# Sparse attention in batches of two key tiles, with the tensor engine's half-row work kept together

## The chip, the core and the metric

The kernel runs on one core of a Trainium2 chip. The metric is device time in microseconds (us), the median of three runs. The kernel before takes 2334.74 us (2334.36 to 2340.01). The profile is one execution of it, 2307.7 us from its first to its last instruction. Engines: PE does matrix products (PEld are its weight loads), DVE and ACT work on vectors, POOL issues the gathers, SP issues plain transfers.

## What is computed

One layer of attention over a graph, followed by a mixture of experts. Cut to what matters here:

```python
# x: 4096 x 512, adj: 4096 x 4096 of 0 and 1, 8 heads of 64
adj = maximum(adj, eye)
q, k, v = (einsum('nd,hdk->hnk', layernorm(x), W) for W in (Wqs, Wks, Wvs))
scores = einsum('hqk,hmk->hqm', q, k) * kd ** -0.5
scores = scores + 0.01 * eye - 1e16 * (1.0 - adj)
att = softmax(scores, axis=-1)
x = x + einsum('hqm,hmk,hko->qo', att, v, Wo)
x = x + experts(layernorm(x))     # the best 2 of 8 experts for each row
```

adj has few ones, unevenly spread. For each tile of 128 queries the kernel lists the keys that any of them uses, packs them into tiles of 128 keys and works only on those. All arithmetic is in float32.

## The kernel before

Stages: projections and lists; attention; the end of the routing; experts. The attention is the stage that the change touches.

A tile of queries has its own tile of keys (c = -1) and listed[i] tiles of listed keys. A listed tile counts for all 128 queries, or for one half of them (64) when its keys are used by that half alone (half_of is None, 0 or 1). A step handles one tile of keys for one tile of queries. Names: `kv` holds keys and values as gathered (128 keys x 1024), `kT` the keys turned so that heads lie on the rows, `s` the scores in PSUM, `e` their exps, `mask` the gathered part of adj, `po` the sum of values, `acc` the sum of exps.

```python
def turn(n):                       # transposes on PE, 64 rows each
    pk = ps_k.tile([P, 2, TB], F32, tag="k")          # ps_k: 1 buffer
    for p in range(NP):                               # NP = 4 pairs of heads
        for r in range(2):
            half = slice(r * KD, (r + 1) * KD)        # KD = 64
            nc.tensor.transpose(pk[:, r, ts(p, KD)], kv[n][half, ts(p, P)], ident[half, half])
    nc.scalar.copy(kT[n]..., pk...)                   # ACT

def scores(n):
    ...
    if full:                                          # 128 queries: 8 products in half rows
        s = [ps_s.tile([P, NP, P], F32, tag="s") for r in range(2)]   # ps_s: 3 buffers
        for p in range(NP):
            for r in range(2):
                rows = slice(r * KD, (r + 1) * KD)
                nc.tensor.matmul(s[r][:, p, :], k[rows, p, :], q_in[i][rows, p, r, :], ...)
        for r in range(2):
            nc.scalar.activation(e..., s[r], AF.Exp)
    else:                                             # 64 queries: 4 products in full rows
        s = ps_s.tile([P, NP, 2, QH], F32, tag="s")   # q_in holds zeros off its diagonal
        for p in range(NP):
            nc.tensor.matmul(s[:, p], k[:, p, :], q_in[i][:, p, :, q], ...)
        nc.scalar.activation(e, s..., AF.Exp)

def masked(n):
    nc.vector.tensor_mul(e, e, m...)                  # DVE

def values(n):
    for h in range(H):                                # 8 products, 128 rows by 64 columns
        p, r = divmod(h, 2)
        nc.tensor.matmul(po[i][r * KD : (r + 1) * KD, p, q], v[:, ts(h, KD)], e[:, h, :], ...)
    if c >= 0:
        nc.vector.tensor_add(acc[i][:, :, q], acc[i][:, :, q], e)

for n, (i, c) in enumerate(items):
    begin()                                           # vector parts of the last step's job
    fetch(n + AHEAD)                                  # AHEAD = 9: kv and mask, 10 buffers
    ...
    if c < 0 and i:
        nc.scalar.copy(osb[i - 1], po.pop(i - 1))     # ps_o: 1 buffer
    turn(n + 3)
    scores(n + 2)                                     # with their exps
    values(n)
    later(n)                                          # pieces of ends of tiles, gate jobs
    masked(n + 2)
```

The ends of a tile (`piece`) are: k=1 `sums` (sums of exps over keys), k=2 their reciprocal, k=3 `rb` (the reciprocals spread to all rows), k=4 the scaled `o`, k=5 `py` (the product with Wo), k=6 the sum with x and its layer norm. Gate jobs, one at a time, turn the row (`pt_b`), multiply it with the gate's weights (`pg`, `pl`), rank the experts and place the rows.

Of the kernel before, what the change touches and what calls it, by code (L numbers as in the profile page):

```python
# [43 lines left out]
def kernel(  # L44
# [165 lines left out]
    AHEAD = 9  # L210
    items = [(i, c) for i in range(NT) for c in range(-1, listed[i])]
# [7 lines left out]
    def load_q(i):  # L219

        q_in[i] = q_two[i % 2]
        for r in range(2):
            rows = slice(r * KD, (r + 1) * KD)
            nc.sync.dma_start(out=q_in[i][rows, :, r, :], in_=qT_d[rows, :, ts(i, P)])
# [8 lines left out]
    def gather_mask(m, i, c):  # L233
        if half_of(i, c) is None:
            gather(m, adjT_rows, mask_of, i, c)
        else:
            gather(m[:, :QH], adjT_halves, mask_of, i, c)
# [4 lines left out]
    def mask_part(m, i, c):  # L242
        return m if half_of(i, c) is None else m[:, :QH]

    def fetch(n):

        i, c = items[n]
        kv[n] = kvp.tile([P, KV], F32, tag="kv", name=f"kv_{i}_{c}")
        mask[n] = kvp.tile([P, P], F32, tag="mask", name=f"mask_{i}_{c}")
        if c < 0:  # L250
            nc.sync.dma_start(out=kv[n], in_=kv_d[ts(i, P), :])
            nc.sync.dma_start(out=mask[n], in_=adjT[i, ts(i, P), :])
            return
        gather(kv[n], kv_d, key_of, i, c)
        if (i, c) in packed:
            nc.sync.dma_start(out=mask_part(mask[n], i, c), in_=packed_at(i, c))
        else:
            gather_mask(mask[n], i, c)

        if waiting and n % 3 == 0:  # L260
            waiting.pop(0)[1]()
# [9 lines left out]
    with tc.tile_pool(name="wqkv", bufs=1) as wp, tc.tile_pool(name="p1", bufs=3) as work, tc.tile_pool(  # L271
# [353 lines left out]
        def pack():  # L625
            i, c = ready.pop(0)
            m = work.tile([P, P], F32, tag="mask", bufs=5, name=f"pm_{i}_{c}")
            gather_mask(m, i, c)
            packed[i, c] = len(packed)
            nc.sync.dma_start(out=packed_at(i, c), in_=mask_part(m, i, c))  # L630
# [4 lines left out]
        for u in range(8 * NTB + 1):  # L635
# [38 lines left out]
            if u - 3 in load_at:  # L674
                neighbours(load_at[u - 3])
                if load_at[u - 3] == NT - 1:

                    ap_cm.__exit__(None, None, None)
                    kv_cm = tc.tile_pool(name="kv", bufs=AHEAD + 1, side="right")
                    kvp = kv_cm.__enter__()  # L680
                    q_cm = tc.tile_pool(name="q", bufs=1, side="right")
                    qp = q_cm.__enter__()
                    q_two = [qp.tile([P, NP, 2, P], F32, name=f"q_{k}") for k in range(2)]
                    for t in q_two:
                        for r in range(2):
                            rows = slice(r * KD, (r + 1) * KD)
                            nc.gpsimd.memset(t[rows, :, 1 - r, :], 0.0)
                    load_q(0)
                    fetch(0)
            if u == 8 * NTB - 4:  # L690
                for n in range(1, AHEAD):
                    fetch(n)
# [172 lines left out]
    with tc.tile_pool(name="p2a", bufs=2) as two, tc.tile_pool(  # L865
# [30 lines left out]
        x_in, kT, es, po, acc = {}, {}, {}, {}, {}  # L896
# [7 lines left out]
        def load_x(i):  # L904
            x_in[i] = two.tile(
                [P, D], F32, tag="last" if i == NT - 1 else "xt", bufs=1, name=f"xr_{i}"
            )
            nc.sync.dma_start(out=x_in[i], in_=x[ts(i, P), :])

        def turn(n):  # L910
            kT[n] = work.tile([P, NP, P], F32, tag="kT", bufs=3, name=f"kT_{n}")

            pk = ps_k.tile([P, 2, TB], F32, tag="k", name=f"pk_{n}")
            for p in range(NP):
                for r in range(2):
                    half = slice(r * KD, (r + 1) * KD)
                    nc.tensor.transpose(  # L917
                        pk[:, r, ts(p, KD)], kv[n][half, ts(p, P)], ident[half, half]
                    )
            nc.scalar.copy(  # L920
                kT[n].rearrange("k p (r j) -> k r p j", r=2),
                pk[:, :, : NP * KD].rearrange("k r (p j) -> k r p j", p=NP),
            )
# [4 lines left out]

        def scores(n):

            i, c = items[n]
            full = half_of(i, c) is None
            q = queries(i, c)
            k = kT.pop(n)
            if c < 0:
                e = two.tile([P, H, P], F32, tag="acc", name=f"acc_{i}")
                acc[i] = e
            else:
                e = work.tile([P, H, P], F32, tag="e", name=f"e_{i}_{c}")
                if not full:  # L940
                    e = e.rearrange("p h q -> p (h q)")[:, : H * QH]
                    e = e.rearrange("p (h q) -> p h q", h=H)
            es[n] = e
            if full:

                s = [
                    ps_s.tile([P, NP, P], F32, tag="s", name=f"s{r}_{i}_{c}") for r in range(2)
                ]
                for p in range(NP):
                    for r in range(2):  # L950
                        rows = slice(r * KD, (r + 1) * KD)
                        nc.tensor.matmul(  # L952
                            s[r][:, p, :], k[rows, p, :], q_in[i][rows, p, r, :],
                            start=True, stop=True,
                        )
                for r in range(2):
                    nc.scalar.activation(  # L957
                        e.rearrange("p (a r) q -> p r a q", r=2)[:, r], s[r], AF.Exp
                    )
            else:  # L960

# [490 lines left out]
```

## Time and profile before

| part | value |
|---|---|
| median of 3 runs | 2334.74 us |
| span in the profile | 2307.7 us |
| PE busy in the span | 2102.1 us (91%) |
| DVE, ACT, POOL busy | 1266.7, 933.3, 1030.9 us |
| projections and lists | 0 to 462 us |
| attention | 462 to 1693 us |
| end of the routing | 1693 to 1760 us |
| experts | 1760 to 2307.7 us |

How to read it: a row of the profile names the line of the kernel, the engine, the operation, what is written and what is read, and the shape. L917 are the transposes, L920 their copy, L952 the scores of 128 queries and L964 those of 64, L957 and L967 the exps, L975 the mask, L987 the values, L993 the sum of exps, L1012 `sums`, L1025 `rb`, L1034 `py`, L702, L708 and L721 the gate's products, L1150 the copy of `po`, L228 the gathers. "64*128" ahead of a shape is the part of PE's array that is used, rows by columns. A float32 product appears as two records of a load and a matmul each, a transpose as one. The end of a matmul is modelled, so distances between starts tell more than durations. The granted clock is PE's, as a share of its full speed.

### The profile page before, as it was taken

How to read it: one execution, taken by the hardware profiler on the slowest of the kernel's cores; microseconds unless marked ns; L12 is line 12 of the kernel's file. 1: busy time of each engine (PE TensorE's matmuls, PEld its weight loads, DVE VectorE, ACT ScalarE, POOL GpSimd, SP SyncE). 2: the span in 40 equal slices, each digit the busy share in tenths (PEclk: the TensorE clock that was granted, in tenths of full speed). 3: DMA queues.
4: the chain of work that ended last, by engine and by line, in shares of the span. 5: the costliest groups of instructions: out<-in, count | busy, mean ns of one | idle time of the engine just before them, and what ended most of it. 6: DMA issues, size and time to landing. Idle time of an engine off the chain costs nothing. (4 is left out here: it accounts for less than half of the span.)

```text
span 2307.7 us, 48617 instructions
## 1 busy us (share of the span) xinstructions
PE 2102.1 (91%) x18796; PEld 1389.0 (60%) x18796; DVE 1266.7 (55%) x2297; ACT 933.3 (40%) x1709; POOL 1030.9 (45%) x1080
## 2 busy tenths in 40 slices
PE   7988897899999889999999999998957999999998
PEld 3434443387777777777777777776733444444444
DVE  4686676166666656656656666665652332323332
ACT  2644443355445445445445454544421222222221
POOL 1044434667666566565555655566521121212112
PEclk9998999899999999999899999999978999999999
DMA  7777877667777777778777877767666656665564
GB/s 293 313 264 269 273 261 248 207 192 212 225 242 233 221 235 234 220 219 234 211 234 223 237 220 225 224 197 225 186 237 148 134 137 136 137 138 134 137 132 91
DMA packets 214383, 481.13 MB, mean 208 GB/s; under 512 B 49234, under 2 KB 81234, under 8 KB 210052
## 3 DMA queue, kind: packets, MB, share of 16 engines
q0 software_dynamic: 79232, 242.18, 37.1%
q1 hardware_dynamic: 133764, 233.68, 33.0%
q8 instruction: 153, 2.51, 0.4%
q10 hardware_dynamic: 1152, 2.10, 0.3%
q14 instruction: 82, 0.67, 0.1%
HBM read 400.43 MB, written 77.42 MB: 207 GB/s over the span
## 5 line engine op out<-in xcount | busy, mean ns | idle before, releaser
L228 POOL DMA_INDIRECT kv<-kv_d,key_of x363 | 405.8, 1118 | 384.4 <-PE po L987 220.5
L975 DVE TENSOR_TENSOR e<-e,mask 128x512 f32<-128x512 f32 (+1 forms) x363 | 322.3, 888 | 308.1 <-ACT e L967 144.3
L920 ACT COPY kT<-pk 128x512 f32<-128x512 f32 x395 | 232.3, 588 | 370.6 <-PE pk L917 216.6
L987 PE MATMUL po<-e,kv 128*64 128x64 f32 (+1 forms) x5808 | 322.4, 250 | 18.2 <-issue 17.9
L1387 POOL DMA_INDIRECT out_dram<-y,r x71 | 110.6, 1558 | 473.7 <-ACT y L1386 453.2
L993 DVE TENSOR_TENSOR acc<-acc,e 128x512 f32<-128x512 f32 (+1 forms) x363 | 320.5, 883 | 2.5 <-PE sums L1012 0.9
L228 POOL DMA_INDIRECT mask<-in_adjT_dram,mask_of x234 | 282.3, 1206 | 72.9 <-issue 63.4
L987 PEld LDWEIGHTS po<-e,kv 128*64 128x64 f32 x5808 | 251.9, 139 | 70.1 <-issue 25.8
L964 PE MATMUL s<-q,kT 128*128 128x128 f32 x1832 | 276.2, 295 | 3.1 <-issue 2.7
L1351 PE MATMUL ph<-w,xT 128*128 x568 | 257.9, 597 | 0.7 <-ACT xT L207 0.7
L1380 PE MATMUL py<-w,hT 128*128 x568 | 255.6, 593 | 0.9 <-DVE hT L1365 0.9
L964 PEld LDWEIGHTS s<-q,kT 128*128 128x128 f32 x1832 | 230.8, 197 | 19.4 <-issue 3.5
L917 PE MATMUL pk<-ident,kv 64*128 64x64 f32 x2904 | 177.5, 239 | 49.0 <-ACT kT L920 30.1
L917 PEld LDWEIGHTS pk<-ident,kv 64*128 64x128 f32 x2904 | 123.9, 141 | 120.2 <-issue 72.0
L228 POOL DMA_INDIRECT pm<-in_adjT_dram,mask_of x129 | 126.2, 978 | 149.6 <-DMA packed_h<-pm 80.0
L957 ACT ACTIVATE e<-s 128x512 f32<-128x512 f32 x268 | 146.9, 597 | 72.1 <-PE s L952 30.1
L1385 DVE TENSOR_TENSOR y<-py,bb 128x512 f32<-128x512 f32 x71 | 49.1, 692 | 225.6 <-PE py L1380 225.6
L967 ACT ACTIVATE e<-s 128x512 f32<-128x512 f32 x229 | 137.9, 602 | 79.4 <-PE s L964 43.9
L359 DVE TENSOR_REDUCE flags<-adjT 128x64 f32<-128x4096 f32 x32 | 141.0, 4408 | 52.3 <-DMA adjT<-in_adjT_dram 52.3
L1351 PEld LDWEIGHTS ph<-w,xT 128*128 128x128 f32 x568 | 103.1, 192 | 103.8 <-issue 102.7
L1380 PEld LDWEIGHTS py<-w,hT 128*128 128x128 f32 x568 | 102.5, 190 | 104.0 <-issue 102.8
L952 PE MATMUL s<-q,kT 64*128 64x128 f32 x2144 | 160.2, 283 | 4.6 <-issue 2.6
(598 smaller groups left out, 2614.8 us busy)
## 6 DMA issues: line engine op xcount, KB each, us to landing
adjT<-in_adjT_dram SPq DMA_DIRECT2D x32, 2048.0 KB
bb<-in_L_ffn_b_dram SPq DMA_DIRECT2D x142, 256.0 KB
r<-xs_d SPq DMA_DIRECT2D x71, 258.0 KB
kv_d<-kv SPq DMA_DIRECT2D x32, 512.0 KB
xt<-in_x_dram SPq DMA_DIRECT2D x32, 256.0 KB
qT_d<-qT SPq DMA_DIRECT2D x8, 1024.0 KB
q<-qT_d SPq DMA_DIRECT2D x64, 128.0 KB
xr<-in_x_dram SPq DMA_DIRECT2D x32, 256.0 KB
```

What stands on the lines that cost most here:

```text
L228: nc.gpsimd.indirect_dma_start(out=to, out_offset=None, in_=src, in_offset=bass.IndirectOffsetOnAxis(ap=of[:, at[i] + c : at[i] + c + 1], ...
L359: nc.vector.tensor_reduce(flags[g][:, :, j, :], adj_in.pop(i).rearrange("p c (h q) -> p h c q", h=2), axis=AX.X, op=ALU.max,)
L917: nc.tensor.transpose(pk[:, r, ts(p, KD)], kv[n][half, ts(p, P)], ident[half, half])
L920: nc.scalar.copy(kT[n].rearrange("k p (r j) -> k r p j", r=2), pk[:, :, : NP * KD].rearrange("k r (p j) -> k r p j", p=NP),)
L952: nc.tensor.matmul(s[r][:, p, :], k[rows, p, :], q_in[i][rows, p, r, :], start=True, stop=True,)
L957: nc.scalar.activation(e.rearrange("p (a r) q -> p r a q", r=2)[:, r], s[r], AF.Exp)
L964: nc.tensor.matmul(s[:, p], k[:, p, :], q_in[i][:, p, :, q], start=True, stop=True)
L975: nc.vector.tensor_mul(e, e, m.unsqueeze(1).to_broadcast(e.shape))
L987: nc.tensor.matmul(po[i][r * KD : (r + 1) * KD, p, q], v[:, ts(h, KD)], e[:, h, :], start=(c < 0 and p == 0), stop=(c == listed[i] - 1), s ...
L993: nc.vector.tensor_add(acc[i][:, :, q], acc[i][:, :, q], e)
L1351: nc.tensor.matmul(ph, xTs[b][:, c, :], w1[:, bass.ds(es[b], 1), c, :], start=(c == 0), stop=(c == DC - 1),)
L1380: nc.tensor.matmul(py, hTs[b][:, c, :], w2[:, bass.ds(es[b], 1), c, :], start=(c == 0), stop=(c == HC - 1),)
```

## The change

Two tiles of keys form a batch. Two listed tiles for 64 queries each, one for the first half of the queries and one for the second where there are such, become one unit with 128 columns of scores; tiles for 128 queries stay units of one. A batch is one paired unit, or two of the others. PE then changes less often between products in half rows (transposes, scores) and in full rows or columns (values, ends of tiles). For that the scores of 64 queries go from four products in full rows with zeros in q to eight in half rows, and q loses its zeros. Two keys share one copy of kT. The copy of po follows the last values of its tile. The core of the diff, with cuts marked:

```diff
-    AHEAD = 9
-    items = [(i, c) for i in range(NT) for c in range(-1, listed[i])]
+    KEPT = 10
+    units, batches = [], []
+    for i in range(NT):
+        parts = {h: [c for c in range(listed[i]) if half_of(i, c) is h] for h in (0, None, 1)}
+        pairs = [[a, b] for a, b in zip(parts[0], parts[1])]
+        ...
+        wide = [[-1]] + [[c] for c in parts[None]]
+        ...
+        wide = [wide[j : j + 2] for j in range(0, len(wide), 2)]
+        pairs = [[pair] for pair in pairs]
...
-        def turn(n):
-            kT[n] = work.tile([P, NP, P], F32, tag="kT", bufs=3, name=f"kT_{n}")
+        def turn(batch):
+            k = work.tile([P, 2, NP, P], F32, tag="kT", bufs=2, name=f"kT_{batch[0]}")
+            ...                      # transposes of both keys, then one copy on ACT
...
         def scores(n):
+            for r in range(2):
+                s = ps_s.tile([P, NP * P], F32, tag="s", name=f"s{r}_{n}")
+            for j, c in enumerate(cs):
+                for p in range(NP):
+                    for r in range(2):
+                        rows = slice(r * KD, (r + 1) * KD)
+                        nc.tensor.matmul(
+                            ss[n][r][:, p, ts(j, m)], k[rows, p, :],
+                            q_in[i][rows, p, queries(i, c)], start=True, stop=True,
+                        )
-                for p in range(NP):
-                    nc.tensor.matmul(
-                        s[:, p], k[:, p, :], q_in[i][:, p, :, q], start=True, stop=True
-                    )
...
         def values(n):
+            if last:
+                osb[i] = single.tile([P, NP, P], F32, tag="o", name=f"o_{i}")
+                nc.scalar.copy(osb[i], po.pop(i))
...
-        LAST = 6
+        LAST = 4                     # products of k=1, 2, 3 in later(b); their reads in begin(b)
...
-        for n, (i, c) in enumerate(items):
-            begin()
-            fetch(n + AHEAD)
-            turn(n + 3)
-            scores(n + 2)
-            values(n)
-            later(n)
-            masked(n + 2)
+        for b, batch in enumerate(batches):
+            begin(b)
+            fetch(k0 + KEPT)         # k0: the batch's first key
+            ...
+            for n in batch[: 0 if own else None]:
+                summed(n)            # acc, taken out of values
+            for n in nxt:            # the next batch
+                scores(n)
+                exps(n)
+                if n == nxt[0] and b + 2 < len(batches):
+                    turn(batches[b + 2])
+                masked(n)
+            for n in batch:
+                if own:
+                    summed(n)
+                values(n)
+            later(b)
```

The other stages are the same in both kernels.

## The prediction

> **What bounds the kernel now.** I read four views in this order. The table by windows splits the span into stages, with the edges taken from the first and last start of the values' matmuls and of the expert blocks. Columns: stretch, its length, busy time of PE, PEld (weight loads), DVE, ACT, POOL, then granted clock, DMA share, GB/s.
>
> ```profile
> 462.00:1693.00 1231.00, 1142.58 (x15377) 920.43 (x15375) 798.96 (x1243) 606.96 (x1206) 741.17 (x639) 0.97 0.74 219
> 1760.00:2307.70 547.70, 538.21 (x1665) 264.99 (x1663) 165.88 (x348) 127.68 (x208) 110.64 (x71) 1.00 0.58 131
> ```
>
> The first row is the attention, 1231 of 2308 us, and the only stage that the change touches: PE is busy 93% of it, DVE 65%, POOL 60%, ACT 49%. So PE's stream sets the pace, and I go to its timeline for the price of each phase. A phase costs the distance from its start to the start of the next (the printed duration has a tail that overlaps the next phase).
>
> ```profile
> 1109.28 0.69 PE L987 MATMUL po<-e,kv 128*64 128x64 f32 x16
> 1109.90 0.46 PE L917 MATMUL pk<-ident,kv 64*128 64x64 f32 x8
> 1110.29 1.16 PE L964 MATMUL s<-q,kT 128*128 128x128 f32 x8
> 1111.38 0.69 PE L987 MATMUL po<-e,kv 128*64 128x64 f32 x16
> ...
> 1123.89 0.47 PE L917 MATMUL pk<-ident,kv 64*128 64x64 f32 x8
> 1124.19 1.11 PE L952 MATMUL s<-q,kT 64*128 64x128 f32 x16
> 1125.23 0.69 PE L987 MATMUL po<-e,kv 128*64 128x64 f32 x16
> ```
>
> Read off: a step on 64 queries is values 0.62, transposes 0.39, scores 1.09 = 2.10 us. A step on 128 queries has transposes 0.30 and scores 1.04; its values are in the same timeline at 1101.46 with the next phase at 1102.49, so 1.03, together 2.37. There are 229 of the first (363 listed tiles less the 134 whose mask product is 128x1024) and 134 + 32 own tiles = 166 of the second. The ends of a tile, from the same timeline: sums 0.58, rb 1.09, transposes of the output 0.59, gate 0.36 and 0.32; py is 120.1 us busy for 32 tiles, 3.75 each: 6.7 in all. Sum: 229 x 2.10 + 166 x 2.37 + 32 x 6.7 = 481 + 393 + 214 = 1088 us. The stage takes 1231, so **some 143 us are lost** in waits and in stretches at half clock (a phase that follows a long wait takes about twice its usual time). By the waits, PE and its loads wait most for ACT's copy of po (15.5 us, and 19.4 for the loads) and of kT (22.1 and 28.8).
>
> Third, what is fixed in a phase and what grows with the work. Values on 64 columns cost 0.62, on 128 columns 1.03. The loads in the 0.69 us phase start 0.059 us apart per pair (0.55 us less one load's 0.137, over 7 steps), so 8 pairs are 0.47 and 0.15 is fixed. The timeline of the loads gives the scores:
>
> ```profile
> 1108.18 0.19 PEld L952 LDWEIGHTS s_-1_12111<-q,kT 64*128 64x128 f32 x1
> 1108.18 0.19 PEld L952 LDWEIGHTS s_-1_12112<-q,kT 64*128 64x128 f32 x1
> 1108.30 0.19 PEld L952 LDWEIGHTS s_-1_12111<-q,kT 64*128 64x128 f32 x1
> 1108.30 0.19 PEld L952 LDWEIGHTS s_-1_12112<-q,kT 64*128 64x128 f32 x1
> 1108.41 0.19 PEld L952 LDWEIGHTS s_-1_12111<-q,kT 64*128 64x128 f32 x1
> ```
>
> The two halves of the rows load at the same instant, and a new pair comes each 0.11 us: 8 pairs are 0.88. The rest, 0.16 for 128 queries and 0.21 for 64, is fixed. The transposes' loads come 0.06 per pair (0.33 less 0.139, over 3): 0.24 for 4 pairs, so 0.06 is fixed if scores in half rows follow and 0.15 if scores in full rows do. The whole fixed part is then 0.15 + 0.21 + 0.15 = 0.51 us in a step on 64 queries and about 0.37 in one on 128.
>
> **What the Trainium skill says.** "TensorEngine Tiling (Array Packing)", section Tiling Modes, says that a change of tiling mode, not of the tile alone, drains the engine. The trace agrees: the same eight transposes cost 0.39 ahead of full rows and 0.30 ahead of half rows, 0.09 for the drain. "TensorE: Matmul & The Clock Gate", section LDWEIGHTS, puts a load at its columns over 1.2, whatever its rows; for 128 columns 107 ns, and the trace shows 0.11 us a pair. Its section on the clock gate says that a long idle spell halves PE's clock, which fits the mean of 0.97 here and 0.67 in the stretch of waits after this stage. "PSUM — Partial Sum Buffer", section on bank collisions, lets two row tiles not write one bank at a time, which explains why a half-row product takes two of the three score banks.
>
> **The change part by part.** The 395 keys become 207 batches. Counting them with the code: 102 pairs of half tiles in one unit, 78 of two 128-query units (32 with the own tile), 8 mixed, 19 of one key.
>
> *Pair batch, PE alone.* Scores in half rows: 16 matmuls, each of two records, are 16 pairs of records. They now have 64 columns, not 128, but a pair still loads 128 columns of kT, so I keep 0.11: 1.76, plus 0.10 to enter the mode. Eight pairs of transposes 0.48, drain 0.09, values 16 x 0.059 + 0.15 = 1.09. Sum 3.52 against 2 x 2.10 = 4.20: **0.68 saved**, all of it fixed parts. The scores themselves save nothing.
>
> *Pair batch, with ACT.* The new order is scores(b+1), exps(b+1), transposes(b+2), copy kT(b+2), then values(b), and the next scores need that copy. ACT's queue is in order, so the copy waits for both exps. From the start of the last score: 0.30 to the first exp (in the timeline above the last pair starts at 1124.19 + 0.05 + 7 x 0.11 = 1125.01, and ACT's exp stands at 1125.33), then 0.5 from one to the next, as three neighbours on ACT show:
>
> ```profile
> 1109.94 0.60 ACT L957 ACTIVATE acc<-s_-1_12111 128x512 f32<-128x512 f32 x1
> 1110.43 0.59 ACT L957 ACTIVATE acc<-s_-1_12112 128x512 f32<-128x512 f32 x1
> 1110.96 0.59 ACT L920 COPY kT<-pk 128x512 f32<-128x512 f32 x1
> ```
>
> So 0.30 + 1.0, and the copy is 128x1024 now. From 0.27 for 128 elements and 0.59 for 512 I estimate 0.17 + 1024 x 0.83 ns = 1.0, and 0.05 back to PE: 2.35. PE has 0.11 + 0.48 + 0.09 + 1.09 = 1.8 to do meanwhile, so it **waits 0.55** unless ends fill the gap. The gain is 0.1 plus the ends E of that batch, at most 0.68. One third of pair batches (32) carry rb (1.09): 22 us. Gate pieces (0.3 to 0.6) fall in about half of the other 70: 35 x 0.5 = 18. The last 35 give 4. Sum 44.
>
> *Wide batch.* Scores 0.10 + 0.88, transposes 0.48, scores 0.05 + 0.88, drain 0.09, values 16 x 0.109 + 0.15 = 1.89: 4.37 against 2 x 2.37. But the second scores need a fourth bank of three, free only after the first exp: 0.30 + 0.60 + 0.05 = 0.95 after the last score, and PE arrives at 0.65. So 4.67, 0.07 saved, 78 times: 5. Mixed ones give some 3. One-key batches on 64 queries (17) lose about 0.5 to ACT's chain: -8. **Regular part: 44 us off.**
>
> *What else moves.* The copy of po now directly follows a tile's last values, and the next tile's values come a whole scores phase later: the wait of 35 us on PE and its loads should go, and some half clock with it; I take 50 of the 143. DVE gets one product of 1.22 for two of 0.69, twice per pair batch: 0.32 x 102 = 33 us, off the path. Against it: fetches now come two at a time and are needed two batches later, about 11 us, where before they had six steps (6 x 3.1 = 18.7). POOL needs 3.8 us to issue two, DMA some 5 for 1 MB at 219 GB/s. It fits, not by much; and the half tiles' scores have twice the records. I put 20 us on both.
>
> Sum: 44 + 50 - 20 = 74, so 2334.74 - 74 = about 2260.
>
> **The rivals.** (1) *ACT's chain takes all:* with a slower copy or exps held up behind other ACT work, pair batches come to 4.2 or more, and gain and loss cancel: 2300 to 2335. ACT's 49% busy speaks against; the strict order of exps before the copy speaks for. (2) *The loads end behind need:* DMA share 0.74 would become 0.79 at the shorter stage, and the slack falls by 7 us; PE would wait for kv in many batches, 2320 or more. Against it: no wait of PE for a kv transfer is listed now, and POOL is idle 40% of the stage. (3) *PE gets its full saving:* if scores on 64 columns cost less than 0.11 a pair, or ends fill all gaps, regular gain is 102 x 0.68 + 78 x 0.37 = 98, with 50 from waits 148: about 2190.
>
> **Range and chances.** 2260 with 2205 to 2315: the low end is most of rival 3, the high end most of rival 1. The 2% mark is 2288. I give 0.70 for faster, 0.23 within, 0.07 slower; the gain's parts are independent, and two of them would have to fail.
>
> **What would show it.** Half scores at 0.11 us a pair: right if 16 pairs take 1.7 to 1.9. The wait of PE for ACT's kT copy should grow to 20 us or more in total and be the longest of its list; that for the po copy should nearly vanish. The copy should read 1.0 us. DVE should be busy about 30 us less. PE waits for kv would show rival 2. I am wrong if the stage ends above 1210 us (the waits stayed) or under 1090 (scores were cheap).

## The result, and the profile after

The changed kernel takes 2448.21 us (median of 6; 2442.64 to 2465.52) beside 2334.32 us for the kernel before on the same chip (6 runs): a ratio of **1.0509, 95% interval 1.0468 to 1.055**. The ratios, here and below, are those on record, made from the single executions; they differ a little from quotients of the medians. Predicted were 2260 us, 2205 to 2315. The change is slower by 114 us where it should have been 74 faster.

One fact is needed for all that follows. The kernel before took 2305 to 2340 us in this comparison and in three later ones (two of them on one chip), and 2171 to 2190 us in four others, each on a chip of its own; nothing in the kernel differed. I call them the slower and the faster chips, though no run tells whether the chip itself or something else at work on it makes the difference. Every ratio below is to the kernel before on the same chip.

The stage of attention, in the view by windows (window, length, busy us and instructions of PE, its loads, DVE, ACT and POOL, mean granted clock, DMA share, GB/s), now reads:

```profile
464.00:1831.00 1367.00, 1191.06 (x17177) 999.15 (x17175) 787.34 (x1044) 565.35 (x1037) 712.37 (x632) 0.89 0.64 196
```

It was 1231 long at a clock of 0.97; it is 1367 at 0.89. These 136 us, and 18 more between the last values and the first product of the experts (51.4 before, 69.6 after), make up 154 of the 156 us by which the two profiled runs differ (spans of 2307.7 and 2463.6). The timeline of PE shows what happens inside:

```profile
869.89 1.15 PE L1020 MATMUL po<-e,kv 128*64 128x64 f32 x32
870.97 2.00 PE L973 MATMUL s<-q,kT 64*128 64x64 f32 x32
872.81 0.49 PE L937 MATMUL pk<-ident,kv 64*128 64x64 f32 x10
873.70 0.36 PE L937 MATMUL pk<-ident,kv 64*128 64x64 f32 x4 [0.40 <-issue]
874.45 0.28 PE L937 MATMUL pk<-ident,kv 64*128 64x64 f32 x2 [0.39 <-issue]
874.65 1.10 PE L1020 MATMUL po<-e,kv 128*64 128x128 f32 x9
875.97 2.18 PE L1020 MATMUL po<-e,kv 128*64 128x128 f32 x23 [0.21 <-issue]
878.31 3.68 PE L973 MATMUL s<-q,kT 64*128 64x64 f32 x32 [0.15 <-ACT kT L942]
881.77 0.53 PE L937 MATMUL pk<-ident,kv_-1_8366 64*128 64x64 f32 x6
```

The first two lines are as priced: values of two half tiles take 1.08 us to the next phase, 16 pairs of half-row scores 1.84. Then the 16 transposes break into groups of ten, four and two, with idle time in between for which no semaphore accounts ("issue"), and the next two phases take about twice their price: 32 values 3.66 in place of 1.90, and the same 32 scores 3.46 in place of 1.84. The windows over this stretch, cut where the clock can change, show the reason:

```profile
868.92:872.33 3.41, 3.41 (x70) 3.27 (x72) 3.41 (x4) 1.85 (x4) 1.16 (x2) 1.00 0.89 266
872.33:875.75 3.42, 2.51 (x37) 1.72 (x35) 1.10 (x2) 0.00 (x0) 2.81 (x3) 1.00 1.03 314
875.75:879.16 3.41, 3.04 (x32) 2.60 (x33) 1.74 (x2) 2.10 (x3) 1.99 (x2) 0.50 0.64 238
879.16:882.57 3.41, 3.41 (x44) 3.41 (x42) 0.71 (x1) 0.56 (x2) 2.18 (x3) 0.50 0.60 173
882.57:885.99 3.42, 3.42 (x50) 3.19 (x48) 2.65 (x3) 1.43 (x3) 1.52 (x2) 0.50 0.98 289
885.99:889.40 3.41, 2.89 (x48) 2.30 (x46) 1.00 (x1) 1.20 (x2) 2.43 (x3) 1.00 1.03 267
```

The clock is the third number from the end of a line. The slot from 872.33 holds the gaps; PE is busy 2.51 of its 3.41 us. The next three slots run at 0.50. The view of waits for the stage says how much of each there is:

```profile
PE po L1020 <- issue: 58.0, 119, 1.2
PE pk L937 <- issue: 26.9, 55, 1.1
PE s L973 <- ACT kT L942: 23.9, 32, 1.9
PE s L973 <- ACT e L986: 23.0, 27, 2.1
PE s L973 <- issue: 15.0, 29, 2.1
```

Columns: who waits for what, us in total, times, longest. The waits for ACT are those that were foreseen; "issue" comes to 100 us, where before had 42.5 (18.9 + 18.3 + 2.7 + 2.6). Four lines of before:

```profile
PE pk L917 <- ACT kT L920: 22.1, 24, 3.2
PE pk L917 <- issue: 18.9, 41, 1.8
PE po L987 <- issue: 18.3, 48, 1.1
PE po L987 <- ACT o L1150: 15.5, 18, 3.5
```

To have sums, I split PE's stage by its phases: the "own price" is the first decile of the durations of phases of one kind; the excess is put to gaps of over 0.32 us inside the phase, then to half clock (half of the time spent under it), and the rest to waits at a change of phase. All in us; the last two columns are the same kernels on a faster chip (experiment 2).

| | before | after | before, faster chip | after, faster chip |
|---|---|---|---|---|
| own price | 1073 | 1010 | 1076 | 999 |
| gaps inside a phase | 42 | 155 | 1 | 43 |
| half clock | 29 | 122 | 9 | 24 |
| waits at a change of phase | 86 | 74 | 16 | 41 |
| sum | 1230 | 1361 | 1102 | 1105 |
| time under half clock | 68 | 305 | 26 | 79 |

PE's own saving came, 63 us; by the prices of the prediction it should have been some 75 ahead of ACT's wait (102 x 0.68 + 78 x 0.07). Gaps took 113 and half clock 93, together 206. The split depends on how phases and gaps are told apart: with phases grouped by shape and number of records, the own price falls by 91, and gaps and half clock rise by 187 (idle time over 0.32 us) to 226 (distance of two starts over 0.32 us). The gaps of after on the faster chip are of another kind: there no wait on "issue" is listed, and PE's longest waits are for keys.

### The profile page after: what moved, and what is told of

Read it like the earlier page. It is cut to its first block, busy times and chain, and to the rows that moved or that the text cites. A ratio compares the mean times of both kernels' runs of the same rounds, so it can differ in the third digit from the quotient of the medians.

```text
span 2463.6 us, 51175 instructions
## 1 busy us (share of the span) xinstructions
PE 2156.2 (88%) x20628; PEld 1472.5 (60%) x20628; DVE 1257.3 (51%) x2102; ACT 895.4 (36%) x1546; POOL 1008.4 (41%) x1076
## 5 line engine op out<-in xcount | busy, mean ns | idle before, releaser
L973 PE MATMUL s<-q,kT 64*128 64x64 f32 (+1 forms) x6320 | 508.9, 299 | 71.9 <-ACT kT L942 23.9
L973 PEld LDWEIGHTS s<-q,kT 64*128 64x128 f32 x6320 | 447.6, 206 | 129.8 <-issue 46.6
L992 DVE TENSOR_TENSOR e<-e,mask 128x1024 f32<-128x1024 f32 (+1 forms) x261 | 306.3, 1174 | 365.7 <-ACT e L986 332.0
L986 ACT ACTIVATE e<-s 128x512 f32<-128x512 f32 (+1 forms) x522 | 276.1, 581 | 469.1 <-PE s L973 176.3
L1020 PEld LDWEIGHTS po<-e,kv 128*64 128x64 f32 x5808 | 283.9, 152 | 97.1 <-issue 70.5
L248 POOL DMA_INDIRECT mask<-in_adjT_dram,mask_of x234 | 253.3, 1082 | 74.4 <-issue 67.4
L1002 DVE TENSOR_TENSOR acc<-acc,e 128x1024 f32<-128x1024 f32 x227 | 274.9, 1211 | 4.0 <-PE po L1020 1.0
L942 ACT COPY kT<-pk 128x1024 f32<-128x1024 f32 (+1 forms) x207 | 202.5, 978 | 63.0 <-remote 20.2
L1059 PE MATMUL py<-wo,o 128*128 128x512 f32 x256 | 129.5, 653 | 1.6 <-DVE least L1237 0.9
L1433 ACT ACTIVATE y<-y,gate 128x512 f32<-128x512 f32 x71 | 51.2, 722 | 213.5 <-DVE y L1432 213.5
```

The costliest lines, as they stand in the source:

```text
L248: nc.gpsimd.indirect_dma_start(out=to, out_offset=None, in_=src, in_offset=bass.IndirectOffsetOnAxis(ap=of[:, at[i] + c : at[i] + c + 1], ...
L942: nc.scalar.copy(k.rearrange("k j p (r c) -> k r (j p) c", r=2)[:, :, :m], pk.rearrange("k r (m c) -> k r m c", c=KD)[:, :, :m],)
L973: nc.tensor.matmul(ss[n][r][:, p, ts(j, m)], k[rows, p, :], q_in[i][rows, p, queries(i, c)], start=True, stop=True,)
L986: nc.scalar.activation(heads(es[n])[:, r], ss[n][r], AF.Exp)
L992: nc.vector.tensor_mul(es[n], es[n], m)
L1002: nc.vector.tensor_add(acc[i], acc[i], es[n])
```

## The experiments

**1. More and fewer PE instructions.** My first theory was supply: both kernels get the same 25 loads and products (records, below) a us in the stage (30752 in 1231 us, 34352 in 1367), as if PE could have no more. Four kernels change their number.

```diff
b_rows8 (of before): half scores in half rows
-  s[:, p] <- k[:, p, :], q_in[i][:, p, :, q]                 # 4 products, 8 records
+  s[r][:, p, :] <- k[rows, p, :], q_in[i][rows, p, r, q]     # 8, 16 records; r = 0, 1
a_full4 (of after): half scores in full rows
-  ss[n][r][:, p, ts(j, m)] <- k[rows, p, :], q_in[i][rows, p, queries(i, c)]
+  s[:, p] <- k[:, p, :], q_in[i][:, p, :, queries(i, c)]     # 4, q with zeros; an exp for each key
b_turn4, a_turn4: keys turned in full rows
-  8 transposes of [half, ts(p, P)] a key
+  4 transposes of [:, ts(p, P)] a key
```

> Kernel before, its order kept; only the scores on 64 queries are taken in 16 half-row products of 64 columns (8 pairs) where before took 8 full-row ones: 229 keys x 8 = 1832 more matmuls and as many more weight loads. Supply theory (PE gets about 25.15 records per us in the attention stage, in before 31079 in 1231 us and in after 34382 in 1367 us): 34743 records, stage about 1381 us, total about 2480. Rival, PE's own prices: a step on 64 queries saves about 0.2 us of mode change and exps come in two halves, total about 2290 to 2340. Rival, batch order or ACT's chain is what cost time in after: this kernel has neither, total within 2% of 2335.

> Kernel after, its batches kept; only the scores on 64 queries go back to 8 full-row products on q with zeros, as in before (3664 PE records fewer than after; 8 buffers for masks in place of 10). Supply theory: records as in before or a little under, stage about 1225 to 1250 us, total about 2310 to 2345. Rival, batch order or ACT's chain (copy of kT behind two exps, exps that now end later): total stays at 2440 or above, since the number of mode changes grows as well.

> Kernel before; kv is turned by 4 full-row transposes of 128x128 a key in place of 8 half-row ones of 64x128: 395 x 8 = 3160 PE records fewer. Supply theory: (31079 - 3160) / 25.15 = 1110 us for the stage, total about 2215, unless another limit comes first. PE-price theory: 4 full-row pairs at 0.11 in place of 4 half-row pairs at 0.06 cost 0.2 us a key more, less a mode change of 0.09 for the half steps: total 2335 to 2400.

> Kernel after; kv is turned by 4 full-row transposes a key (3160 PE records fewer), which breaks the long half-row stretch with a change of mode. Supply theory: 31222 records, stage about 1241 us, total about 2335 or less. Rival, batch order, ACT's chain or mode changes: total stays at 2440 or goes above 2480.

They fell on a faster chip (before 2176.27 us): b_rows8 2161.3, ratio 0.9937 (0.9913 to 0.996); a_full4 2192.63, 1.0093 (1.0062 to 1.0123); b_turn4 2210.76, 1.0166 (1.014 to 1.0191); a_turn4 2241.9, 1.0307 (1.0275 to 1.0339). The supply theory had no such chip in it. b_rows8 gets 31.7 records a us here (34479 in 1089 us), and only the prices of PE show: the half-row scores take 0.98 us ahead of values where full-row ones take 1.09, and full-row transposes cost more than half-row ones. What a total of 2335 means had to be asked first.

**2. The two kernels on one of these chips, and a pair with equal PE time.** The transposes done twice, against one more product of 240 columns into a free part of their bank.

```diff
b_dup:   -  for p in range(NP):
         +  for p in [*range(NP), *range(NP)]:
b_long:  +  matmul(pk[:, 0, 256:496], kv[n][:KD, :P], wo[:KD, 0, :240])
```

> The kernel before, unchanged, for a profile on the same chip as the next runs: in the last experiments it took 2176 us where it took 2334 us beside the kernel after. Supply theory: where it takes about 2335 its trace shows gaps of 0.4 to 0.5 us inside phases of PE (88 counted before), where it takes about 2176 next to none, with the prices of the phases the same in both. Rival, another kernel-wide cause (clock, memory): the phases themselves are longer in the slow one, or other stages than attention differ as well.

> The kernel after, unchanged. Supply theory: where before takes about 2335, after takes about 2450 again; where before takes about 2176, no supply limit holds and after gains what its phases promised, some 60 to 80 us of PE's own prices less a few for new waits: 2110 to 2150, ratio about 0.98. Rival, order of batches or ACT's chain: after is 4 to 5% slower than before whatever before takes.

> Kernel before with the 8 transposes of every key done twice into the same place: 6320 PE records more, 395 x 0.24 = 95 us more of PE's own time. Supply theory where before takes 2335: (31079 + 6320) / 25.15 = 1487 us for the stage, total about 2590, 255 more than before. PE-price theory, and supply theory where before takes 2176 (31 records a us would be needed, and 31.8 were had): 95 more than before, about 2270.

> Kernel before with one more product of 240 columns a key, into a free part of the transposes' bank: the same PE time as the doubled transposes (395 x 0.22 = 87 us), but 790 records in place of 6320. Supply theory where before takes 2335: between 0 and 90 us more than before, far under the doubled transposes. PE-price theory, and supply theory where before takes 2176: 85 to 95 more than before, as the doubled transposes.

before_2 took 2174.0 us; after_2 2201.2, **ratio 1.0114 (1.0097 to 1.013)**; b_dup 2276.24, 101 us more where 95 were priced. b_long took 2342.06: its product costs 0.42 us (167 / 395) where I took 0.22, so the pair says nothing. The price was wrong by a factor of two: a float32 product is two records, and the timeline of b_long has both, 240 columns each. The records of py, 512 columns each, start 0.43 us apart; two of 240 columns come to 0.40 by that. The stage of the two kernels on the faster chip:

```profile
455.00:1559.00 1104.00, 1085.57 (x15406) 886.25 (x15406) 802.49 (x1259) 617.56 (x1208) 739.22 (x646) 0.99 0.80 246
455.00:1572.00 1117.00, 1033.82 (x17203) 891.94 (x17203) 783.83 (x1063) 557.61 (x1039) 740.60 (x641) 0.96 0.76 243
```

The prices of the phases are the same as on the slower chip, but before has one idle spell of PE over 0.32 us inside a phase where it had 51, and after 19 where it had 148. With the gaps gone, the change still loses. The waits of before_2, then of after_2:

```profile
PE pk L917 <- ACT kT L920: 17.2, 8, 7.9
PE po L987 <- ACT o L1150: 5.3, 2, 3.0
PE pt_b L702 <- ACT rows L200: 1.8, 5, 0.4
```

```profile
PE pk L937 <- DMA kv<-kv_d,key_of: 23.9, 11, 12.2
PE s L973 <- ACT kT L942: 21.1, 30, 1.2
PE s L973 <- ACT e L986: 9.5, 15, 3.4
PE po L1020 <- DVE e L992: 8.6, 2, 5.1
PE pk L937 <- ACT kT L942: 8.1, 1, 8.1
PE s L973 <- ACT acc L986: 6.5, 4, 2.1
```

24 us of waits are replaced by 83 (the six longest are shown): late loads, ACT's copy, banks of scores that wait for exps, and values that wait for the mask.

**3. ACT's chain, and the end of the stage.** a_mid puts the copy of kT between the two exps of a unit; a_all is a_mid with two routing jobs a batch in the last nine batches.

```diff
a_mid:  -  exps(n)                       # both, then turn(b + 2) with its copy
        +  exps(n, 0); turn(batches[b + 2]); exps(n, 1)
a_all:  +  for k in range(2 if b >= len(batches) - 9 else 1):
               ...                       # one job of routing
```

> Kernel after with ACT's queue changed: the copy of kT stands between the two exps of a unit, not behind both. Theory ACT's chain (the strict order of both exps ahead of the copy is what eats PE's saving): the copy ends 0.5 us sooner and PE's 21 us wait for kT, 30 on its loads, goes: 20 to 30 us less than the kernel after, that is about 2175 where after takes 2201, 2420 where it takes 2448. Rival, the waits lie with loads and the end of the stage: within 8 us of the kernel after.

> The same with, in the last nine batches, two routing jobs a batch in place of one. Theory that the end of the stage costs 16 us because one job a batch, with batches of two keys, leaves a group of routing over: 12 to 20 us less than the kernel with the copy in the middle alone, and the time from the last values to the first expert product falls from 67 to about 51. Rival, that time is the chain of the last tile whatever is left over: unchanged within 5 us.

> The kernel before with half-row scores once more, which has 34740 PE records in the stage. Supply theory, with a limit that differs between chips: where before takes about 2335 (its rate stood at 25.1 records a us), the stage takes 34740 / 25.15 = 1381 us and the total is about 2480; where before takes 2175, 2160 as in the first run of it. Rival, the 2335 are owed to something that costs each kernel the same: 1 per cent under before on any chip.

On a faster chip again: a_mid 2225.06 us, ratio 1.0227 (1.0186 to 1.0269), that is slower than the kernel after; a_all 2220.72, 1.0203 (1.0179 to 1.0227); b_rows8_2 2160.4, as before. The waits of a_mid:

```profile
PE s L973 <- ACT e L985: 28.4, 20, 4.3
PE pk L937 <- DMA kv<-kv_d,key_of: 26.4, 17, 11.8
...
PE s L973 <- ACT kT L942: 8.5, 15, 1.4
```

The wait for the copy fell from 21.1 to 8.5 us, and that for a bank of scores rose from 9.5 to 28.4: the second scores of a wide batch took 157.8 us in all where they had taken 132.5. ACT's order can give to pair batches only what it takes from wide ones. In a_all the time from last values to first expert product fell from 67.7 to 51.9, as expected, and the last values came 12.7 later: the jobs were moved, and the 4 us between the two kernels are within the noise, where 12 to 20 were expected. Two jobs a batch don't win the longer end back.

**4. Eight times the transposes.**

```diff
b_dup8:  -  for p in range(NP):
         +  for p in [*range(NP)] * 8:
```

> Kernel before with the 8 transposes of every key done eight times into the same place: 7 x 395 x 16 = 44240 PE records more (75319 in all in the stage), each eight of them 0.25 us by the run with the doubled ones: 691 us more if only PE's prices count, about 2865 where before takes 2175, at 42 records a us. Supply theory: there is a ceiling on the records that PE gets per us, it lies above the 31.8 had so far on chips where before takes 2175; if it lies at 36 the stage takes 75319 / 36 = 2092 us and the total is about 3165, with gaps of 0.4 to 0.5 us inside the transposes as in the trace of after. Where before takes 2335, at a ceiling of 25 to 28, 75319 / 25.15 = 2995 us for the stage, about 4090 in total; a cause that isn't supply would give about 3025 there.

This one fell on a slower chip, with before at 2325.79 us (one execution of each): 3059.78 us, where supply said 4090 and "a cause that isn't supply" 3025. PE got 75070 records in 1989 us, 38 a us, on a slower chip; before gets 25 on such a one. **The theory of a mean supply is refuted.** The gaps are there all the same:

```profile
457.00:2446.00 1989.00, 1868.47 (x37535) 1623.65 (x37535) 810.79 (x1262) 624.78 (x1211) 727.22 (x650) 0.99 0.46 139
```
```profile
PE pk L917 <- issue: 102.7, 271, 2.6
```

**5. Bursts or traffic.** If not the mean, perhaps bursts: half-row scores leave no slow phase. Or the gathers' traffic. a_full4_2 is a_full4 unchanged; a_keys gathers 2 KB a key and not 4, and its keys serve as values too.

```diff
a_keys:  -  gather(kv[n, j], kv_d, key_of, i, c)
         +  gather(kv[n, j][:, : H * KD], <kv_d as rows of half the length>, key_of, i, c)
         -  v = kv.pop((n, j))[:, H * KD :]
         +  v = kv.pop((n, j))[:, : H * KD]
```

> The kernel after with half scores in full rows once more. Burst theory (beside a before of 2330): full-row scores ask for 17 PE records a us where half-row ones on 64 columns ask for 35, so the buffer fills again between the transposes and values, which ask for 55: gaps inside phases fall from 250 to 100 or so, total 2330 to 2370, some 80 to 120 less than the kernel after. Rival, the gathers' traffic or the batch order makes the gaps: as the kernel after, 2430 or more. Beside a before of 2175: 2190, as in its first run.

> The kernel after with each gathered key's row cut to half its bytes (2 KB in place of 4), which serve as keys and values alike; so half of the gathers' traffic and of the data is left out. Traffic theory, beside a before of 2330: with half the traffic most gaps inside phases go, 100 us or more under 2448. Burst theory with a supply that doesn't depend on traffic: within 20 us of 2448. Beside a before of 2175, theory that late loads are part of the loss: PE's wait for kv transfers (24 us) goes, and 25 to 35 us with it, 2165 to 2177; rival, ACT's chain would take up the time at once: 2195 or more.

Slower chip, before 2317.1 us. a_full4_2: 2356.05 us, ratio 1.0171 (1.0142 to 1.0201), so two thirds of the loss are gone; where the two kernels took 2201.2 and 2192.63, the intervals overlap. The edit has other parts, which no run separates: each key's exp needs that key's four products alone, so ACT can begin sooner, and the masks have 8 buffers in place of 10. a_keys: 2433.89 us, 1.0507 (1.0459 to 1.0555): half of the gathers' bytes changed nothing, so their volume is out. But a_full4_2 keeps much of its gaps: 70 us of "issue" are listed, 101 in after, and 106 idle spells over 0.32 us inside phases for 148; the burst theory had them fall to 40%. What differs more is the clock, 0.95 for 0.89 and 0.90:

```profile
455.00:1710.00 1255.00, 1112.15 (x15367) 931.82 (x15369) 786.38 (x1052) 578.38 (x1014) 721.55 (x632) 0.95 0.69 214
455.00:1800.00 1345.00, 1174.77 (x17203) 981.71 (x17203) 786.84 (x1053) 567.08 (x1039) 718.52 (x638) 0.90 0.44 130
```

In the trace of b_dup8, too, the mean clock of the stage is 0.99 (34 us of 1989 at half clock), with 271 waits for nothing listed. So gaps alone don't bring half clock; something in what PE does between them decides.

**The clock, read from the traces.** Every change of the clock lies on a grid of 3.413 us that runs through the whole trace. For each slot of the grid in the attention stage I summed the work of the products that start in it, as rows x columns x columns streamed, with full-array records of 512 columns back to back (0.454 us each: eight of py in 3.64 us) as 100%. The slots of the fence above come to

```
slot from   PE busy   work   clock of the slot   clock of the next
868.92        3.41     57%         1.00                1.00
872.33        2.51     35%         1.00                0.50
875.75        3.04     32%         0.50                0.50
879.16        3.41     33%         0.50                0.50
882.57        3.42     47%         0.50                1.00
```

In the attention stages of the 20 profiled runs, 273 slots at full clock had under 38.5% of work, and 255 of them were followed by a slot at half; of 6405 with more, 13 were. A slot at half clock does half the work, and the same limit holds there: of 223 such slots under it 221 were followed by another, of 297 above it 27. The limit is a fit. But set on the traces of before and after alone (39.5%), it puts 39 of the 6436 slots of the other 18 wrong, and the best limit on PE's busy time from the same two traces puts 214 wrong. Only products whose sizes the records give could be counted, so the stage of the experts is not in this. "TensorE: Matmul & The Clock Gate" of the Trainium skill, section The HAM clock gate, has the 3413 ns and that they run freely, and the traces agree. Its rule against idle gaps over 3.4 us (section HAM oscillation) doesn't reach these cases: of the 268 full-clock slots that were followed by half clock, half had PE busy for 48% or more, one for 90%. Some idle time there always was: of 5073 slots at full clock with PE busy for over 3.3 us none was followed by half. The slot from 879.16 is busy all the time and stays at half because its clock is half already.

By the same measure the phases are worth, in one us: transposes 76%, values on 64 columns 74%, full-row half scores 83% (the zeros count), and **half-row scores on 64 columns 46%** (16 x 64 x 1/2 columns in 0.98 us), for the load of 128 weights sets their time and 64 columns don't fill it. In after, two keys of them follow one another: 1.84 of 3.41 us near the limit, but above it, and it takes some gaps in the rest to push the slot under it.

**6. The same instructions, twice the work.** This asks for a kernel with the number, order and price of after's instructions and more work. A load of 128 weights leaves time to stream 128 columns; so each half-row product streams 128 columns of q, and the 64 that aren't wanted are overwritten by the next or not read.

```diff
a_wide (of after):
-  q_in[i][rows, p, queries(i, c)]            # 64 columns; products in the order j, p, r
+  q[rows, at_q : at_q + 128]                 # q_in[i] flat, cut off at its end; order p, j, r
b_rows8w (of b_rows8):
-  q_in[i][rows, p, r, q]                     # 64 columns
+  q_in[i][rows, p, r, :]                     # 128; the exp reads the 64 of q
```

> The kernel after, with each half-row product of the half scores streaming 128 columns of q in place of 64; the second 64 results are overwritten by the next product or not read. The number of PE records and their price (0.11 us a pair, set by the load) stay, the work by rows x columns doubles. Clock theory: stretches at half clock fall from 305 us in the stage to 100 to 150 beside a before of 2320 to 2335, total 2360 to 2400 in place of 2448; beside a before of 2175 from 75 to about 40 us, total 2180 to 2190 in place of 2201. Rival, the number of instructions: the total stays within 10 us of the kernel after on either.

> The kernel before with half scores in half rows, each product streaming all 128 queries of which 64 are read. Clock theory: beside a before of 2175 a little under the 2161 of the same with 64 columns, 2145 to 2160, with half the stretches at half clock (68 us); beside a before of 2320 to 2335 about as far under it, 2300 to 2330. Rival, the number of instructions (34740 records, more than in the kernel after): beside a before of 2320 to 2335, 2430 or more; beside 2175, 2161 as with 64 columns.

On a slower chip, with before at 2317.14 us: a_wide 2418.8 us, ratio 1.0406 (1.0348 to 1.0465); b_rows8w 2333.4, 1.0083 (1.0053 to 1.0112). One of a_wide's four executions, at 2447.44 us, fell in a slower state of the core and is left out of its ratio; with it the quotient of the medians is 1.044, where that of after is 1.049. The stage of a_wide, then of b_rows8w:

```profile
455.00:1786.00 1331.00, 1152.91 (x17203) 963.32 (x17203) 788.99 (x1056) 566.91 (x1039) 717.76 (x640) 0.93 0.66 203
455.00:1703.00 1248.00, 1154.47 (x17223) 933.03 (x17223) 800.67 (x1261) 627.11 (x1437) 729.02 (x645) 0.97 0.74 218
```

b_rows8w settles the number of instructions: 34446 records in the stage, more than after's 34352, on a chip with gaps, and 0.8% over before where after is 5.1% over it. a_wide goes the way of the clock theory but falls short of it: time under half clock fell from 305 to 194 us (100 to 150 expected), with as many idle spells inside phases (153 for 148); the ratio fell by 0.010, some 24 us, and the total stayed above the 2360 to 2400 expected. In the traces, work sets the clock. How much time that is rests on these 24 us, and the two intervals all but touch; they are not the whole of the 79 us (0.0338 x 2334) that full-row scores win.

b_rows8w and a_wide have the same kind of half-row scores on the same chip and differ in the rest of the change: one key at a time, or batches with their shared copy of kT and early copy of po. Batches cost 0.032 of before there, some 75 us: idle spells inside phases are 66 in one and 153 in the other, time under half clock is 67 us and 194 (68 in before).

**7. What was left beside a faster chip.** a_keys_2 and b_rows8w_2 are a_keys and b_rows8w unchanged.

> The kernel after with half the gathered bytes (keys serve as values), once more, for a before of 2175. Theory that late loads are part of the loss: PE's wait for kv transfers (24 us) goes, and 25 to 35 us with it, 2165 to 2177 where after takes 2201. Rival, ACT's chain takes up the time at once: 2195 or more. Beside a before of 2320: 2434, as in its first run.

> The kernel before with half scores in half rows, each product streaming all 128 queries, once more, for a before of 2175. Clock theory: stretches at half clock fall under the 68 us of the one with 64 columns, 2145 to 2160. Rival, the clock was not what held that one back: 2161 or more. Beside a before of 2320: 2333, as in its first run.

Before took 2185.32 us. a_keys_2: 2202.27, ratio 1.0081 (1.0057 to 1.0106), which overlaps with 1.0114 (1.0097 to 1.013) of after. Half the bytes won next to nothing, and PE still waits 18.5 us for keys, 10.0 of them at one place. In after_2 that place is at 1507 us: POOL issues three scatters of the routing at 1502.8, 1507.9 and 1513.5, waiting some 4 us ahead of each, and the next gather stands behind them in its queue, at 1514.8. There it is the queue, not the transfer, that makes a load late. b_rows8w_2: 2157.3 us, **0.987 (0.985 to 0.989)**, beside 0.9937 with 64 columns; the time under half clock went from 75 to 26 us, and 16 records of scores now cost 1.040 us for 0.986, 12 us over 229 keys:

```profile
455.00:1544.00 1089.00, 1063.74 (x17240) 890.12 (x17239) 799.21 (x1250) 630.64 (x1437) 751.16 (x640) 0.97 0.81 249
455.00:1536.00 1081.00, 1055.30 (x17230) 871.40 (x17232) 800.48 (x1261) 631.49 (x1438) 753.44 (x645) 0.99 0.81 252
```

(b_rows8, then b_rows8w_2.) This is the best version found: it beats both kernels on the faster chips, and lies 0.8% behind before on the slower ones. No version was best on both. All ratios to before by the order of work and by how the half scores are done:

| | full rows | half rows, 64 columns | half rows, 128 columns |
|---|---|---|---|
| slower chips, one key at a time | 1 | not run | 1.0083 |
| slower chips, batches | 1.0171 | 1.0509 | 1.0406 |
| faster chips, one key at a time | 1 | 0.9937, 0.9928 | 0.987 |
| faster chips, batches | 1.0093 | 1.0114 | not run |

In every column that has both, batches lose: about 1 to 2% on the faster chips and 2 to 3% on the slower ones. Half rows win in the old order on the faster chips; the large loss needs batches, half rows and a slower chip together.

**What stays open** is what makes the gaps on the slower chips. They aren't the mean number of PE instructions (38 a us were had), nor the mean traffic (139 GB/s in b_dup8 and 130 in a_keys, with gaps; 246 in before_2, without). That PE is fed in pieces at times isn't excluded: in b_dup8, of 111 gaps that follow another within 1 us, 92 have 10 to 12 records in between. Gaps and waits at changes of phase, less those of the same kernel on a faster chip, come to 9% of the stage in before (111 of 1230 us), 11% in after (145 of 1361), 9% in a_full4_2 (115 of 1247), 11% in a_keys (141 of 1330) and 12% in b_rows8w (148 of 1246): a share of time, nearly whatever runs. "Runtime: NRT & Kernel Launch" of the Trainium skill, section Instruction fetch mechanics, has fetches in blocks of 256 instructions that are mostly hidden; the page of after counts 167 of 16 KB, 135 of them in the stage, one for 254 of PE's records, which agrees. The gaps keep no distance to them: half begin within 3.9 us of the end of the last fetch, and of times picked at random half do within 4.3. I can't name their source, nor say why batches have more of them, and no edit here could test the chip.

## Why the prediction was wrong, by its own steps

- *What bounds, 1088 us of own prices:* right. By phases the own price is 1073 us in before. But the 143 us lost were put to waits of this kernel, to be had by a better order; 111 of them are there on the slower chips alone, which no order of batches took away, and on a faster chip before loses only 26 in all.
- *Fixed parts, 0.68 saved a pair batch:* right. Half scores at 0.11 us a pair: 1.84 us for 16 pairs, between 1.7 and 1.9. Transposes 0.59, values 1.08. PE's own price fell by 63 us in the split, on the faster chip by 77, where these parts and the wide batches promised 75.
- *ACT's chain, 0.55 a pair batch:* right in its mechanism: the copy reads 0.98 to 1.02 us for 1.0, PE's scores wait 23.9 us for it, over the 20 set as the mark, though the mark says little, for before's transposes waited 22.1 for their copy already. It isn't the longest of the list, for "issue" is, and the wait for exps is as long. The wait for a bank in wide batches was under-sized: their second scores cost 1.44 to 1.80 us ahead of values (0.93 + 0.30 + 0.09 = 1.32 foreseen); 76 of them took 132.5 us on the faster chip, 32 more than that. The regular gain of 44 shrank by these.
- *Minus 50 for po's copy and what follows:* this step failed. The wait for that copy is gone, as foreseen, but it was 15.5 us of PE, and what I counted with it was not its doing; waits at changes of phase went from 86 to 74, and from 16 to 41 on the faster chip. The term is -12 where I had -50.
- *Plus 20 for late fetches and twice the records:* this step failed too, and is the term that was mis-sized most: in its place stand 206 us by the split (187 to 226 by the other groupings), 113 of gaps and 93 of half clock. I had priced half-row scores by time alone. They bring PE near the limit of work below which its clock is halved: what cost before 29 us at half clock cost after 122. And I had taken the batches to cost nothing but late fetches; with the same kind of scores they cost 75 us on a slower chip. What is measured: full rows, with their exps by key, win 79 of the 119 us (0.0509 x 2334), and 128 columns some 24. How the 206 divide between the gaps of the slower chips (34 more than in before), after's own waits and the clock is my split, and why the gaps grow with batches stays open.
- *Not in the sum:* the end. Fewer steps leave a group of routing over, and the stage ends 16 to 18 us later; DVE waits 13 us for scatters that still read slot_i (second line), and PE behind it. Both lines are after_2's, where the stage ends 16 us later; in after PE waits 16.20 at this place:

```profile
1611.62 0.19 PE L772 MATMUL pp<-chosen,below 128*128 128x8 bf16 x1 [12.79 <-DVE chosen L756]
```
```profile
1609.24 0.17 DVE L799 CAST slot_i<-slot 128x2 int32<-128x2 f32 x1 [13.14 <-DMA xs_d<-rows,slot_i]
```

- *DVE, 30 us less:* masks and sums fell from 643 to 610 us in the stage, the 33 as priced; the page has DVE only 9 lower in all (1257.3, 1266.7 before). Off the path.
- *Rival 1, ACT's chain takes all:* on the faster chips it is near the truth, together with late loads and the end; 2300 to 2335 was a ratio of 0.985 to 1.0, and it is 1.011. *Rival 2, loads:* in after no wait for keys is listed; on the faster chip 24 us are, and half of them, 12.2, come through POOL's queue and not through DMA. *Rival 3, PE's full saving:* PE had its saving in its phases, and waits and half clock took all of it.

## What to carry to other kernels

Price a phase in work as well as in time. A product in half rows, with fewer columns than its load leaves time for, kept PE busy here at 46% of its work, little above the 38 to 40% under which the clock of the next 3.4 us was halved; then idle time of under 1 us in a slot was enough. Where a product is bound by its load, streaming the columns for which there is time anyway cost 0.054 us for 16 records and took the time at half clock from 75 to 26 us. Change the order of work and the form of the products in separate kernels first: here one lost by itself, the other won by itself on the faster chips, and the two together lost most. And before time "lost in waits" is entered as a gain, ask for each wait which semaphore ends it: where the trace says that the engine waited for nothing, a new order of the work has nothing to win.

## What was not expected of the hardware

- One and the same kernel took 2171 to 2190 us in four comparisons and 2305 to 2340 in four others, each comparison on one chip. Of the 135 us between two profiled runs, 127 lie in the attention, in gaps of PE, mostly of 0.3 to 0.5 us, and what follows from them; the stage of the experts took 562 and 564 us.
- The clock for a slot of 3.413 us followed from the work of the slot before, by rows, columns and columns streamed, better than from the time busy: 39 of 6436 slots wrong for 214. The limit lies near 39% of full-array float32 products.
- Half-row scores of 64 and of 128 columns differ by 0.054 us in 16 records (0.986 and 1.040): the load sets most of their time.
